# How densely the recurrence is issued beside attention and beside feed-forward

## The chip, the cores and the metric

The kernel runs on one core of a Trainium2 chip. The metric is the device time of one execution in microseconds (us); less is better. The core has five engines that work side by side, each through its own queue in order: TensorE (PE; its weight loads are listed as PEld), VectorE (DVE), ScalarE (ACT), GpSimd (POOL) and SyncE (SP), which here only issues transfers. They wait for one another by semaphores.

## The reference

Eight images of 384 channels and 32 x 32 pixels pass through two layers. Cut to what matters:

```python
# layer 0, for each batch, in both directions of the 1024 pixels
u, z   = split(rmsnorm(x) @ in_proj)
u      = silu(causal_conv4(u))
dt, Bm, Cm = split(u @ x_proj)
delta  = softplus(dt @ dt_proj + bias)
h      = exp(delta * A) * h + delta * u * Bm      # the recurrence, 16 states a channel
y      = (sum over states of h * Cm + u * D) * silu(z)
x      = x + res_scale * (scale_mod * (fwd + bwd) @ out_proj
                          + sigmoid(depthwise3x3(xn)) * xn)
# layer 1
t = t + attention(layernorm(t))                   # 6 heads, causal, 1024 tokens
t = t + feed_forward(layernorm(t))                # 384 -> 1536 -> 384, batches 0 to 4 only
```

The feed-forward scales its hidden values by the largest absolute value of the whole group (here one batch) before the GELU, and its output once more in the same way. So all hidden values of a batch must be there before the first GELU, and the GELUs before the second product.

## The kernel before

Everything is in float32, with channels on the 128 partitions (three blocks of 128) and the 1024 pixels or tokens along the free dimension, in two halves of 512. Four kinds of work are issued:

- **Preparation** of a batch (`before_scan`): norm, input projection (L342), the four-tap convolution, the 3 x 3 depthwise convolution on VectorE (`local`, L401), SiLU, the small projection (L489), and `delta` (L513 to L537), which ends with spilling delta and delta x u to DRAM. In `delta` the VectorE lines are L529 to L532.
- **The recurrence**, cut into 768 units, 96 a batch. A unit is one batch, one channel block, one direction and half, and two of the 16 states. `slot(k)` issues the stages of several units, each at its own lead: loads of rows (tile `bc`) and of `ud` and `dl`; `s_first` (GpSimd, L592) writes g = ud x B; `s_scan` has ScalarE make da = exp(delta x A) (L605), VectorE scan it (L610), and GpSimd multiply by C (L616); `s_sum` adds the states up in PSUM by eight transposes on TensorE (L624); `s_gate` finishes a block (L662 to L674). There are six g buffers; a unit's buffer comes free after its transposes. The GpSimd instructions are pinned to program order.
- **Attention** of a batch (`attention`): out-projection of the recurrence's result (L699), layernorm, projections (L729, L747), scores (L787), softmax, transposes (L863), weighted values (L877), projection (L937). It needs all 96 units of its batch.
- **Feed-forward** (`feed_forward`): layernorm, 24 half products of the first layer (`hp`, L995), `quant_scale` (L963 and around it), GELU and clamp (L1018, L1021), 6 half products of the second (`yp`, L1039), `quant_scale` again, the output.

The order of the batches is 0, 1, 2, 3, 5, 6, 4, 7; the first four and batch 4 have a feed-forward. The opening prepares the first four batches beside the first batch's units. Then comes the list `rest`: attention 0, feed-forward 0 joined with the preparation of batch 5, attention 1, feed-forward 1 joined with that of batch 6, and so on with 4 and 7; attention 5, attention 6, attention 4, and the feed-forward of 4 alone. The last attention runs by itself at the end.

Every step carries an assumed duration. `spread_over` merges two lists in proportion to these: each step stands at its middle, as a share of its list's total. The merged steps of a joint feed-forward are then multiplied by `JOINT`. The running sum of durations over `rest` is the planner's time. The units' slots are placed on it: `due` says by which planned time how many slots must be out, and from each point the planner takes the steepest line to any later due point and spaces the slots evenly along it. So a step that counts longer gets more slots beside it.

What is emitted in this order goes through a scheduler that may move instructions on each engine where data and buffers allow it, with a preference for the order of emission; a `high_priority` block goes ahead by the number it names, and pinned instructions keep their order among themselves. Which instruction stands where on an engine is settled before the run.

Of the kernel before, what the change touches and what calls it, by code (L numbers as in the profile page):

```python
# [38 lines left out]
BC0 = 32  # L39
DW = BC0 + 2 * NS  # L40
PARTS = ((0, 0), (0, 1), (1, 1), (1, 0))
JOINT = 0.6
SET = 8
HURRY = 400
AHEAD = 2
# [9 lines left out]
def kernel(  # L55
# [31 lines left out]
    def btile(name):  # L87
        return big.tile([P, NC, L], F32, name=name, tag="big")

    def mtile(name, n=L):  # L90
        return mid.tile([P, n], F32, name=name, tag="mid")
# [7 lines left out]
    def bank(name, tag=None):  # L99
        if tag is None:  # L100
            turn[0] += 1
            tag = ("s", "pt")[turn[0] % 2]
        return ps.tile([P, HB], F32, name=name, tag=tag, bufs=BANKS[tag])

    def half(h):
        return slice(h * HB, (h + 1) * HB)

    def chunk(c):
        return slice(c * P, (c + 1) * P)

    def load(dst, src):
        nc.sync.dma_start(out=dst, in_=src)
# [168 lines left out]
    def layernorm(src, name, emit):  # L281

        dst = src
        st = {}
        for h in range(NH):

            @emit.of(6.0)
            def _(h=h):
                mean = mean_of(lambda c: src()[:, c, half(h)], f"mean_{name}_{h}")
                for c in range(NC):  # L290
                    nc.vector.tensor_tensor(
                        dst()[:, c, half(h)], src()[:, c, half(h)], mean, ALU.subtract
                    )
                st[h] = squares(dst(), h, name)

        for h in range(NH):

            @emit.of(6.0)
            def _(h=h):
                var = mean_of(lambda c: st[h][c], f"var_{name}_{h}")  # L300
                rstd_of(var, 1)
                for c in range(NC):
                    nc.vector.tensor_tensor(  # L303
                        dst()[:, c, half(h)], dst()[:, c, half(h)], var, ALU.mult
                    )
# [652 lines left out]
    def quant_scale(mx, name):  # L958

        col = small.tile([P, 1], F32, name=f"col_{name}", tag="col")  # L960
        nc.vector.tensor_reduce(col, mx, AX.X, ALU.max)
        row = bank(f"row_{name}", "s")
        nc.tensor.transpose(row[:, :P], col.to_broadcast([P, P]), ident)  # L963
        s = small.tile([P, 1], F32, name=f"qs_{name}", tag="qs")
        nc.vector.tensor_reduce(s, row[:, :P], AX.X, ALU.max)
        nc.vector.tensor_scalar(s, s, QEPS, 1.0 / QMAX, ALU.add, ALU.mult)
        nc.vector.reciprocal(s, s)
        return s

    def feed_forward(b, t, emit):  # L970
        st = {}

        @emit
        def _():
            st["xn"] = t()
            st["mxh"] = small.tile([P, NF], F32, name=f"mxh_{b}", tag="mxh", bufs=1)
            st["mxy"] = small.tile([P, NC], F32, name=f"mxy_{b}", tag="mxy", bufs=1)

        layernorm(t, f"nf_{b}", emit)
        for m in range(NF):  # L980
            for h in range(NH):

                @emit.of(3.1)
                def _(m=m, h=h):
                    if m % NC == 0 and h == 0:
                        st["h", m // NC] = btile(f"h{m // NC}_{b}")
                    if m % 2 == 0 and h == 0:
                        st["w1"] = mtile(f"w1_{b}_{m}").rearrange("p (c e) -> p c e", c=4)
                        load(
                            st["w1"][:, :NC, :],  # L990
                            w1s[:, m * P : (m + 2) * P].rearrange("(c p) e -> p c e", p=P),
                        )
                    hp = bank(f"hp_{b}_{m}_{h}", "s")
                    for c in range(NC):
                        nc.tensor.matmul(  # L995
                            out=hp,
                            lhsT=st["w1"][:, c, chunk(m % 2)],
                            rhs=st["xn"][:, c, half(h)],
                            start=(c == 0),
                            stop=(c == NC - 1),  # L1000
                        )
                    hm = st["h", m // NC][:, m % NC, :]
                    nc.scalar.activation(hm[:, half(h)], hp, AF.Identity, bias=b1t[:, m : m + 1])
                    if h == NH - 1:
                        nc.vector.tensor_reduce(
                            st["mxh"][:, m : m + 1], hm, AX.X, ALU.max, apply_absolute_value=True
                        )

        @emit.of(3.0)
        def _():  # L1010
            st["s1"] = quant_scale(st["mxh"], f"h_{b}")


        @emit.of(3.0)
        def _():
            with tc.high_priority(offset=60):
                for q in range(NF // NC):
                    pin(nc.scalar.activation(st["h", q], st["h", q], AF.Gelu, scale=st["s1"]))  # L1018
                pin(nc.scalar.preload_act_table_set(LOG_EXP))
                for q in range(NF // NC):  # L1020
                    nc.vector.tensor_scalar(st["h", q], st["h", q], QCLIP, None, ALU.min)  # L1021

        for m in range(NC):
            for h in range(NH):

                @emit.of(10.7)
                def _(m=m, h=h):
                    if m == 0 and h == 0:
                        st["y"] = btile(f"yf_{b}")
                    if h == 0:  # L1030
                        for k in range(0, NF, 6):
                            w = mtile(f"w2_{b}_{m}_{k}", 6 * P).rearrange("p (k e) -> p k e", k=6)
                            load(
                                w, w2s[k * P : (k + 6) * P, chunk(m)].rearrange("(k p) e -> p k e", p=P)
                            )
                            st["w2", k // 6] = w
                    yp = bank(f"yp_{b}_{m}_{h}", "s")
                    for k in range(NF):
                        nc.tensor.matmul(  # L1039
                            out=yp,  # L1040
                            lhsT=st["w2", k // 6][:, k % 6, :],
                            rhs=st["h", k // NC][:, k % NC, half(h)],
                            start=(k == 0),
                            stop=(k == NF - 1),
                        )
                    ym = st["y"][:, m, :]
                    nc.scalar.activation(
                        ym[:, half(h)], yp, AF.Identity, bias=vec[:, m, V_B2 : V_B2 + 1]
                    )
                    if h == NH - 1:  # L1050
                        nc.vector.tensor_reduce(
                            st["mxy"][:, m : m + 1], ym, AX.X, ALU.max, apply_absolute_value=True
                        )

        @emit.of(3.0)
        def _():
            st["s2"] = quant_scale(st["mxy"], f"y_{b}")

        for m in range(NC):

            @emit
            def _(m=m):
                to = mtile(f"t3_{b}_{m}")
                load(to, spilled[b, "t2", m])
                for h in range(NH):
                    ym = bank(f"yq_{b}_{m}_{h}", "s")
                    nc.vector.tensor_scalar(
                        ym, st["y"][:, m, half(h)], st["s2"], QCLIP, ALU.mult, ALU.min
                    )
                    th = to[:, half(h)]  # L1070
                    nc.vector.scalar_tensor_tensor(th, ym, -QCLIP, th, ALU.max, ALU.add)
                nc.sync.dma_start(out=out[b, chunk(m), :], in_=to)


    class Steps(list):
# [4 lines left out]

        def of(self, us):
            return lambda f: self(f, us)

    def spread_over(*lists):

# [30 lines left out]
    def steps_of(stage, *args, **kwargs):  # L1116
        out = Steps()
        stage(*args, out, **kwargs)
        return out
# [30 lines left out]
    for i, b in enumerate(ORDER):  # L1150
        if i > 0:
            due.append((sum(us for _, us in rest), i * per))
        fed = Steps()
        rest += steps_of(attention, b, fed) if i < B - 1 else []
        if fed and later:
            fed = spread_over(fed, steps_of(before_scan, later.pop(0), ("pt", "pt", "av")))
            fed = [(f, JOINT * us) for f, us in fed]
        rest += fed

    timed, here = [], 0  # L1160
# [63 lines left out]
```

## Time and profile before

| what | us |
|---|---|
| median of 3 runs (lowest, highest) | 4947.52 (4943.62, 4969.08) |
| the profiled execution, its span | 4952.38, 4950.6 |
| PE, DVE, ACT, POOL busy in the span | 4007.3, 3659.0, 2669.5, 3696.7 |
| POOL L592 and L616, 768 each | 1843.2 and 1821.0 |
| DVE L610, 1536 scans | 907.5 + 953.7 |
| opening, up to the first L699 | 0 to 830 |
| first four periods, from one batch's L699 to the next batch's | 658, 675, 670, 682 |
| the last attention | from 4741 to the end |

The profile shows one execution. Busy time is the time in which an engine had an instruction at work; the rest is idle, and for each idle stretch the profile names the instruction or transfer whose end let the engine go on. Matmuls overlap each other on TensorE, so that its busy time is not its real load. "xN" counts instructions or, in a window, those at work in it; most TensorE products in float32 appear as two records each.

### The profile page before, as it was taken

How to read it: one execution, taken by the hardware profiler on the slowest of the kernel's cores; microseconds unless marked ns; L12 is line 12 of the kernel's file. 1: busy time of each engine (PE TensorE's matmuls, PEld its weight loads, DVE VectorE, ACT ScalarE, POOL GpSimd, SP SyncE). 2: the span in 40 equal slices, each digit the busy share in tenths (PEclk: the TensorE clock that was granted, in tenths of full speed). 3: DMA queues.
4: the chain of work that ended last, by engine and by line, in shares of the span. 5: the costliest groups of instructions: out<-in, count | busy, mean ns of one | idle time of the engine just before them, and what ended most of it. 6: DMA issues, size and time to landing. Idle time of an engine off the chain costs nothing. (4 is left out here: it accounts for less than half of the span.)

```text
span 4950.6 us, 50616 instructions
## 1 busy us (share of the span) xinstructions
PE 4007.3 (81%) x16362; PEld 2168.0 (44%) x16362; DVE 3659.0 (74%) x4818; ACT 2669.5 (54%) x4855; POOL 3696.7 (75%) x1944
## 2 busy tenths in 40 slices
PE   4677786988788788688887888887887988988889
PEld 1243343544444444344443444443454444444444
DVE  6887878677887778786778967687867677676623
ACT  4565655564654655545655446565456365464425
POOL 0487787996878986768876699867799888888800
PEclk7787796999989899888898998898899989989999
DMA  6554546333454334363343634334643334334210
GB/s 228 204 177 165 196 157 238 107 102 124 150 198 137 115 124 165 126 207 114 108 135 128 220 121 135 111 128 153 203 128 119 114 112 140 117 103 139 92 61 26
DMA packets 365009, 696.35 MB, mean 141 GB/s; under 512 B 30104, under 2 KB 88904, under 8 KB 364744
## 3 DMA queue, kind: packets, MB, share of 16 engines
q1 hardware_dynamic: 355232, 676.97, 41.4%
q10 hardware_dynamic: 9512, 16.15, 0.9%
q8 instruction: 129, 2.11, 0.2%
q14 instruction: 136, 1.11, 0.1%
HBM read 527.33 MB, written 165.68 MB: 140 GB/s over the span
## 5 line engine op out<-in xcount | busy, mean ns | idle before, releaser
L592 POOL TENSOR_TENSOR g<-ud,bc 128x1024 f32<-128x1024 f32 x768 | 1843.2, 2400 | 518.7 <-PE y L624 391.9
L616 POOL TENSOR_TENSOR g<-g,bc 128x1024 f32<-128x1024 f32 x768 | 1821.0, 2371 | 271.1 <-DVE g L610 196.1
L605 ACT ACTIVATE da<-dl,amat 128x512 f32<-128x512 f32 x1536 | 1056.9, 691 | 1457.7 <-DVE g L610 1436.7
L610 DVE TENSOR_TENSOR_SCAN g<-da,g 128x512 f32<-128x512 f32 x768 | 907.5, 1211 | 423.5 <-POOL g L592 411.8
L610 DVE TENSOR_TENSOR_SCAN g<-da,carry,g 128x512 f32<-128x512 f32 x768 | 953.7, 1272 | 348.4 <-POOL g L592 322.9
L624 PE MATMUL y<-ident,g 128*128 128x128 f32 x6144 | 938.7, 301 | 249.2 <-POOL g L616 122.2
L624 PEld LDWEIGHTS y<-ident,g 128*128 128x128 f32 x6144 | 782.0, 155 | 696.7 <-issue 379.8
L787 PE MATMUL s<-k,q 64*128 64x512 f32 (+3 forms) x1152 | 388.4, 600 | 121.6 <-DVE nm L801 103.5
L801 DVE CUSTOM_DVE_ANT_0 pr<-s,cmask 128x512 f32<-128x512 f32 (+3 forms) x576 | 300.3, 546 | 168.4 <-PE s L787 167.1
L811 ACT ACTIVATE pr<-pr,nm 128x512 f32<-128x512 f32 (+3 forms) x576 | 349.9, 609 | 123.6 <-DVE nm L801 121.9
L863 PE MATMUL pt<-ident,pr 128*128 128x128 f32 x1728 | 301.9, 307 | 98.1 <-ACT ptn L866 78.5
L995 PE MATMUL hp<-t,w 128*128 128x512 f32 x720 | 335.7, 611 | 38.7 <-DMA w<-w1s 30.8
L1039 PE MATMUL yp<-h,w 128*128 128x512 f32 x720 | 331.7, 619 | 19.2 <-DMA w<-w2s 15.1
L863 PEld LDWEIGHTS pt<-ident,pr 128*128 128x128 f32 x1728 | 216.2, 154 | 240.2 <-ACT ptn L866 134.5
L877 PE MATMUL av<-ptn,v 128*64 128x512 f32 (+3 forms) x1152 | 270.8, 551 | 49.7 <-ACT ptn L866 35.8
L342 PE MATMUL in<-xn,win 128*128 128x512 f32 x576 | 282.7, 637 | 26.8 <-DVE xc L464 8.2
L866 ACT COPY ptn<-pt 128x512 f32<-128x512 f32 (+3 forms) x576 | 255.6, 474 | 62.0 <-PE pt L863 60.0
L401 DVE SCALAR_TENSOR_TENSOR loc<-xn,vec,loc 128x496 f32<-128x496 f32 (+3 forms) x384 | 259.6, 722 | 20.1 <-ACT loc L390 18.8
L729 PE MATMUL qp<-t,wqk 128*128 128x512 f32 x576 | 263.3, 607 | 10.3 <-DVE t L303 6.5
L615 POOL COPY carry<-g 128x2 f32<-128x2 f32 x384 | 85.7, 223 | 214.8 <-DVE g L610 214.6
L787 PEld LDWEIGHTS s<-k,q 64*128 64x128 f32 x1152 | 132.2, 207 | 257.9 <-DVE nm L801 174.9
L1039 PEld LDWEIGHTS yp<-h,w 128*128 128x128 f32 x720 | 141.8, 201 | 194.0 <-issue 169.8
(151 smaller groups left out, 4714.2 us busy)
## 6 DMA issues: line engine op xcount, KB each, us to landing
bc<-rows SPq DMA_DIRECT2D x512, 512.0 KB, 4.2
dl<-sdl SPq DMA_DIRECT2D x160, 256.0 KB, 3.0
ud<-sud SPq DMA_DIRECT2D x160, 256.0 KB, 2.8
t<-st SPq DMA_DIRECT2D x63, 512.0 KB, 5.0
su<-u SPq DMA_DIRECT2D x48, 512.0 KB, 4.0
du<-su SPq DMA_DIRECT2D x96, 256.0 KB, 3.9
sdl<-du SPq DMA_DIRECT2D x96, 256.0 KB, 2.6
sud<-du SPq DMA_DIRECT2D x96, 256.0 KB, 2.2
```

The lines of the kernel that those rows point to most:

```text
L342: nc.tensor.matmul(out=mp, lhsT=st["win", c][:, k, i, :], rhs=st["xn"][:, k, half(h)], start=(k == 0), stop=(k == NC - 1),)
L592: pin(nc.gpsimd.tensor_tensor(g, ud, sst["bc", 0, u.b, u.part, u.n], ALU.mult))
L605: nc.scalar.activation(da, sst["dl", u.b, u.c, u.part], AF.Exp, scale=amat[:, u.c, n : n + 1])
L610: nc.vector.tensor_tensor_scan(gi[:, ::step], da[:, ::step], gi[:, ::step], first, ALU.mult, ALU.add)
L616: pin(nc.gpsimd.tensor_tensor(g, g, sst["bc", 1, u.b, u.part, u.n], ALU.mult))
L624: nc.tensor.matmul(out=y[:, j, :], lhsT=g[:, i, chunk(j)], rhs=ident, is_transpose=True, start=(u.opens and i == 0 and j == 0), stop=(u.cl ...
L787: mm = nc.tensor.matmul(out=ss[e][:, : k1 - k0], lhsT=st["q"][rows_of(e), c, chunk(qi)], rhs=st["k"][rows_of(e), c, k0:k1], start=True, st ...
L801: nc.vector.tensor_tensor_reduce(out=x, in0=ss[e][:, :w], in1=mask, scale=-1.0, scalar=-MASKED, op0=ALU.add, op1=ALU.min, accum_out=m,)
L811: nc.scalar.activation(x, x, AF.Exp, bias=m, scale=-1.0, accum_out=rs[:, i, e, kb : kb + 1])
L863: nc.tensor.transpose(pt[:, chunk(i)], pr[:, e, chunk(j % QT)], ident)
L995: nc.tensor.matmul(out=hp, lhsT=st["w1"][:, c, chunk(m % 2)], rhs=st["xn"][:, c, half(h)], start=(c == 0), stop=(c == NC - 1),)
L1039: nc.tensor.matmul(out=yp, lhsT=st["w2", k // 6][:, k % 6, :], rhs=st["h", k // NC][:, k % NC, half(h)], start=(k == 0), stop=(k == NF - 1),)
```

## The change

The factor on a joint feed-forward, `JOINT`, goes from 0.6 to 1.0. Three steps of the feed-forward, the two `quant_scale` calls and the GELU with its clamp, get the durations 9, 16 and 9 us in place of 3 each, and are marked as `Gap`. In `spread_over`, which merges the preparation of a later batch with the feed-forward, the longer durations count. After that merge a `Gap` step counts `SHORT` = 3.0 us for the slots. The last feed-forward, which has no preparation beside it, is not multiplied, and there the steps keep 9, 16 and 9 us. Nothing of what is computed changes.

```diff
-JOINT = 0.6
+JOINT = 1.0
+SHORT = 3.0
...
-        @emit.of(3.0)
+        @emit.of(Gap(9.0))
         def _():
             st["s1"] = quant_scale(st["mxh"], f"h_{b}")
...
-        @emit.of(3.0)
+        @emit.of(Gap(16.0))
         def _():
             with tc.high_priority(offset=60):
                 for q in range(NF // NC):
...
-        @emit.of(3.0)
+        @emit.of(Gap(9.0))
         def _():
             st["s2"] = quant_scale(st["mxy"], f"y_{b}")
...
+    class Gap(float):
+        pass
+
     def spread_over(*lists):
...
         if fed and later:
             fed = spread_over(fed, steps_of(before_scan, later.pop(0), ("pt", "pt", "av")))
-            fed = [(f, JOINT * us) for f, us in fed]
+            fed = [(f, JOINT * (SHORT if isinstance(us, Gap) else us)) for f, us in fed]
         rest += fed
```

## The prediction

> **What bounds the kernel now.** I read the page's slices first, then cut the span into stages, then asked each kind of stage who waits for whom. The slices, in fortieths of the span (124 us each):
>
> ```profile
> PE   4677786988788788688887888887887988988889
> DVE  6887878677887778786778967687867677676623
> POOL 0487787996878986768876699867799888888800
> ```
>
> No engine is full for long, and POOL (GpSimd) swings between 9 and 6 where DVE (VectorE) swings the other way. To see why, I cut where TensorE's timeline has the first out-projection matmul of a batch (L699) and its last attention-projection matmul (L937). From the first to the second I call an A stage (attention), from there to the next L699 an F stage (feed-forward, with a later batch's preparation beside it in the first four). The table by windows; its columns after the length are busy us of PE, PEld, DVE, ACT and POOL, then clock and DMA:
>
> ```profile
> 1488.00:1826.00 338.00, 279.92 (x1364) 159.55 (x1363) 247.97 (x362) 184.03 (x392) 297.21 (x154) 0.91 0.38 126
> 1826.00:2163.00 337.00, 266.17 (x889) 138.25 (x888) 271.50 (x299) 184.30 (x267) 230.74 (x119) 0.88 0.48 156
> 3857.00:4211.00 354.00, 296.45 (x1468) 171.64 (x1467) 250.92 (x366) 185.89 (x391) 319.21 (x167) 0.91 0.37 121
> 4211.00:4524.00 313.00, 267.65 (x1288) 150.86 (x1287) 213.82 (x326) 169.75 (x369) 268.73 (x147) 0.92 0.31 102
> 4524.00:4741.00 217.00, 183.44 (x659) 98.00 (x657) 131.83 (x128) 80.27 (x110) 151.36 (x70) 0.95 0.38 120
> 4741.00:4951.00 210.00, 199.70 (x864) 95.41 (x864) 66.12 (x201) 98.06 (x258) 0.00 (x0) 0.98 0.09 35
> ```
>
> These are A and F of batch 1, A of batches 6 and 4, F of batch 4, and the last batch's attention alone. In A, POOL is busy 297 of 338 us (88%) and DVE 73%. In F, POOL has 231 of 337 (68%) and DVE 81%. The waits of the first two windows say the same; first DVE's longest wait in A, then POOL's waits in F:
>
> ```profile
> DVE g L610 <- POOL g L592: 67.6, 44, 3.0
> ```
> ```profile
> POOL g L592 <- PE y L624: 40.1, 11, 7.1
> POOL carry L615 <- DVE g L610: 31.4, 4, 14.2
> POOL g L616 <- DVE g L610: 26.7, 3, 16.6
> ```
>
> In A the scans wait for POOL: POOL sets the pace. In F POOL waits: 40 us for transposes that free its g buffers, 58 us for scans that stand behind other DVE work, up to 16.6 us at once. So F has room on POOL, little on DVE, and that room is broken up by lumps of DVE work.
>
> The prices of a unit (two states of one channel block):
>
> ```profile
> L592 POOL TENSOR_TENSOR g<-ud,bc 128x1024 f32<-128x1024 f32 x768 | 1843.2, 2400 | 518.7 <-PE y L624 391.9
> L616 POOL TENSOR_TENSOR g<-g,bc 128x1024 f32<-128x1024 f32 x768 | 1821.0, 2371 | 271.1 <-DVE g L610 196.1
> ```
> ```profile
> 4664.52 23.44 PE yp L1039 x54
> 4700.44 1.75 PE y L624 x16
> ```
>
> POOL pays 2.40 + 2.37 us. DVE pays two scans, (907.5 + 953.7) / 768 = 2.42 us (the L610 groups of the page). TensorE's true price is in the chain of waits, where it runs without a pause: 1.75 / 16 = 0.109 us for a transpose, 0.87 us for the eight of a unit; 23.44 / 54 = 0.434 us for a 512-column record of the matmuls.
>
> **What the Trainium skill says.** "Perfetto Trace Analysis", Optimization Strategy: where the most contended engine changes between regimes, interleaving the regimes may help. The two windows above are such regimes. Identifying the Most-Contended Engine, same page: occupancy is a fair measure for the other engines, matmul busy time isn't for TensorE; hence my use of rates there. "SBUF — State Buffer", Who interferes with whom: a DVE operation with two SBUF inputs, or in a two-port mode, and a GpSimd operation that reads SBUF exclude each other; the later one waits for all of the earlier. The trace agrees: L530, with both inputs in SBUF, took
>
> ```profile
> L530 DVE SCALAR_TENSOR_TENSOR dp<-ew x96: 668/701/10682, 113.6 to 3518.9; 128x512 f32<-128x512 f32 x96
> ```
>
> that is 0.67 us at least and 10.7 at most, while L531, with one input in PSUM, never took over 0.69. "TensorE: Matmul & The Clock Gate", What's actually happening: the clock is throttled by default and activity releases it. The windows agree in direction: 0.98 in the last one, 0.88 to 0.91 where TensorE pauses. Denser work doesn't slow it.
>
> **The change, part by part.** It adds and removes no instruction of the computation; it moves units against the rest.
>
> Planner first. An attention counts 306.5 us, a feed-forward 181.6, a preparation 180.2. Before, a joint F counts 0.6 x 361.8 = 217.1. The steepest line to any due point then ends at the seventh batch: 576 / 2707.4 = 0.213 slots per planned us, 0.197 after it. Now a joint F counts 361.8 (the three gap steps 3 each), the steepest line is 672 / 3799.3 = 0.177, throughout. So an A gets 306.5 x 0.177 = 54 slots instead of 65, a joint F 64 instead of 46.
>
> A scheduler reorders afterwards, so I counted in the built order of TensorE, units between the same marks. A: 60, 60, 60, 62, 60, 70, 54 before and 50, 52, 52, 52, 52, 56, 52 after, 60 units fewer in all. F: 50, 52, 50, 52 before, 64, 68, 66, 66 after, 60 more, 15 a stage. The opening (102 units), the last F (36) and the last attention keep their counts. SP's loads of rows, ud and dl move with their units, about 15 more units' worth a joint F; DMA engines are busy 48% there, 38% in A, so I cost that at nothing; the cover goes if the w1 and w2 loads behind them come later than now (24 us of TensorE waits in F of batch 1).
>
> A stages: 7 of them, 2370 us in all (328, 338, 345, 350, 342, 354, 313). Their slope can be read off: 68 firsts on POOL (x of L592) gave 354 us, 57 gave 313, so 41 / 11 = 3.7 us a unit. 60 x 3.7 = 222 us. What is late next is TensorE: attention alone holds it 210 us, 53 units add 53 x 0.93 = 49 (0.87 and a share of the gate's transposes), 259 in stages that would last 307, 84% against 79% now. I take a tenth off: -200 us.
>
> Joint F stages: DVE has 271 us of work, 15 units add 36; POOL goes from 231 to 231 + 15 x 4.77 = 303. Exclusion takes more: L530 and L532 stand 24 times in a joint F, their means of 1.53 and 1.14 us are 0.65 us above the free 0.68; if the excess grows with POOL's share (68% to about 85%) plus clamps (L1021), some 10 us. DVE: 317 us. Its share is now 81%. I let it rise to 88%: in the new DVE order the stretches of over 6 us (by the durations of before) between two scans fall from 104 to 52, 98 to 55 and 104 to 63 us in F of batches 1 to 3 (batch 0 stays at 94), and these are the lumps POOL waits for. 317 / 0.88 = 360, +29 over the mean of 331: +116 us for four. Bounds: at 92%, which single 100 us slices reach, 345 (+14); at today's 82%, 387 (+56).
>
> The gap steps: 34 instead of 9 us of the feed-forward's inner length, so about 30 instead of 9 us of the preparation lie between quantization and GELU. TensorE is half idle there (14.1 of 30 us at 1993 to 2023), but POOL is already busy 27.2 of those 30: more in-projections fit, more units don't. It is part of the 88%. In the last F, without a preparation, the 25 planned us more only shift 36 units: nothing, bounded by -10 and +10.
>
> Sum: -200 + 116 = -84 on the profiled execution's 4952.4 us (span 4950.6): 4868. The median of the runs is 0.1% lower, so 4863; I say 4865.
>
> **Rivals.** *F absorbs nearly all.* For it: POOL idles 100 us in each joint F and the lumps halve. Against: DVE must reach 92%. -222 + 4 x 14 = -166: 4782.
> *A unit costs the same in both.* For it: the opening, also recurrence beside preparation, has POOL at 479 and DVE at 529 of the 630 us from 200 on, 76% and 84%. Against: its lumps are larger. F +52 each: -200 + 208 = +8: 4956.
> *Slower, by DVE's exclusion.* With POOL nearly without pauses, each of the 24 delta operations of a joint F ends behind a whole POOL operation (2.85 us, a length the L530 timeline shows again and again). 24 x (2.85 - 1.33) = 36 us instead of 10, and the scans queued behind them on the in-order DVE come later, and POOL for them: (271 + 36 + 36) / 0.88 = 390, +59 each: -200 + 236 = +36, 4983. It decides from +50 a joint F, that is some 29 us of added waiting. Against: in F of batches 1 and 2 over half of these operations were free.
>
> **How the numbers follow.** Forecast 0.42, own range 4820 to 4905. Absorbed 0.18, equal price 0.18, slower 0.22. The range of eight in ten, 4785 to 4978, takes in the ends 82% and 92% of DVE and leaves about 0.08 below and 0.12 above. A change under 0.5% (25 us) can't be told from none. Faster: 0.42 + 0.18 and a little of the equal price, 0.62; same 0.15; slower 0.23.
>
> **What would show it.** A stages near 310 us with POOL near 82%, and DVE's wait for L592 there well under 67 us; joint F stages near 360 with DVE at 88%, POOL near 84%; L530 mean under 2 us. It is wrong if A stages stay above 325 (then POOL wasn't their pace), or joint F stages pass 380 (then DVE had no room), by longer L530 and L532 or by waits on w1 and w2.

## The result, and the profile after

The changed kernel takes 4954.82 us (median of 8 runs, 4948.57 to 4962.85) against 4946.75 for the kernel before; the ratio is 1.0016, interval 0.9996 to 1.0037. No difference can be told. The profiled execution's span is 4950.7 us, to a tenth that of before. The forecast was 4865. Line numbers from here on are those of the kernel that is named; most of the changed kernel's are one higher than those of before (its L593 is L592 of before, its L617 is L616).

The slices of the page after, three engines:

```profile
PE   4687786988788888778888788887788898988889
DVE  6887878667877778886768786678867666676623
POOL 0487686887887888878878878787788788888700
```

POOL's swings are gone: mostly 7 and 8 where it had been 9 and 6. The work was spread as intended, and the time stayed. The table by windows, cut at the same marks (A and F of batch 1, A of batches 6 and 4, last F, last attention; columns as before):

```profile
1508.00:1832.00 324.00, 271.64 (x1317) 150.32 (x1318) 232.44 (x353) 176.00 (x382) 266.53 (x137) 0.93 0.37 123
1832.00:2189.00 357.00, 285.61 (x995) 154.75 (x993) 299.83 (x321) 208.27 (x302) 301.78 (x149) 0.88 0.50 163
3913.00:4226.00 313.00, 274.69 (x1344) 155.37 (x1343) 211.97 (x336) 170.04 (x367) 258.03 (x139) 0.94 0.38 124
4226.00:4526.00 300.00, 264.77 (x1296) 146.95 (x1295) 201.34 (x319) 165.48 (x367) 256.13 (x138) 0.95 0.30 99
4526.00:4741.00 215.00, 181.27 (x651) 99.06 (x648) 129.72 (x127) 80.78 (x111) 149.92 (x70) 0.92 0.37 119
4741.00:4951.00 210.00, 199.79 (x864) 95.47 (x864) 66.08 (x201) 98.06 (x258) 0.00 (x0) 0.98 0.09 35
```

All stages, from the first L699 start to the last L937 end for A, and from there to the next L699 for F:

| stages | before | after |
|---|---|---|
| A (7) | 331, 345, 354, 358, 342, 342, 320: 2392 | 314, 324, 338, 318, 331, 313, 300: 2238 |
| joint F (4) | 324, 328, 314, 328: 1294 | 363, 358, 370, 367: 1458 |
| last F | 211 | 215 |
| between batches 5, 6 and 4 | 12 | 2 |

A gave 154 us, the joint F stages took 164. In A of batch 1, the longest wait of DVE, then POOL's wait for the transposes that free its g buffers, before and after; last, POOL's waits in F of that batch:

```profile
DVE g L611 <- POOL g L593: 67.1, 41, 4.4
```
```profile
POOL g L592 <- PE y L624: 27.0, 14, 6.0
POOL g L593 <- PE y L625: 40.8, 22, 6.0
```
```profile
POOL carry L616 <- DVE g L611: 16.7, 5, 5.6
POOL g L593 <- PE y L625: 11.6, 6, 3.2
POOL g L617 <- DVE g L611: 11.0, 3, 4.6
```

In F POOL's three waits fell from 98 to 39 us. But POOL's work there rose by 75 (227 to 302 us, cut at the marks of the table), and this stage became 30 us longer. In A DVE waits for POOL as long as before, 67 us, though there are 8 units fewer, and POOL waits longer for TensorE. Over all seven A stages POOL's work fell by 286 us and its waits for the transposes rose from 212 to 340: nearly half of what the units left free came back as a wait for TensorE.

### The profile page after: what moved, and what is told of

It is laid out like the page before. It is cut to its first block, busy times and chain, and to the rows that moved or that the text cites. A ratio compares the mean times of both kernels' runs of the same rounds, so it can differ in the third digit from the quotient of the medians.

```text
span 4950.7 us, 50711 instructions
## 1 busy us (share of the span) xinstructions
PE 4013.9 (81%) x16362; PEld 2162.7 (44%) x16362; DVE 3618.6 (73%) x4808; ACT 2692.7 (54%) x4882; POOL 3696.0 (75%) x1944
## 4 chain that ended last, share of the span: by engine, by line
POOL 35%; PE 20%; DVE 20%; issue 16%; ACT 4%; DMA 4%; SPq 0%; ACTq 0%; POOLq 0%; DVEq 0%
POOL g L593 18%; POOL g L617 16%; DVE g L611 6%; PE qp L730 4%; PE y L625 3%; DVE loc L402 3%; PE yp L1040 2%; DVE dp L531 2%; PE s L788 2%; PE ap L938 2%; PE pt L864 1%; DVE u L371 1%; PE vp L748 1%; PE av L878 1%; DVE du L533 1%
## 5 line engine op out<-in xcount | busy, mean ns | idle before, releaser
L593 POOL TENSOR_TENSOR g<-ud,bc 128x1024 f32<-128x1024 f32 x768 | 1842.6, 2399 | 558.2 <-PE y L625 431.1
L617 POOL TENSOR_TENSOR g<-g,bc 128x1024 f32<-128x1024 f32 x768 | 1823.6, 2375 | 280.7 <-DVE g L611 165.5
L996 PE MATMUL hp<-t,w 128*128 128x512 f32 x720 | 350.1, 633 | 40.7 <-DMA w<-w1s 18.4
L996 PEld LDWEIGHTS hp<-t,w 128*128 128x128 f32 x720 | 137.9, 202 | 201.7 <-issue 146.9
```

The costliest lines, as they stand in the source:

```text
L593: pin(nc.gpsimd.tensor_tensor(g, ud, sst["bc", 0, u.b, u.part, u.n], ALU.mult))
L617: pin(nc.gpsimd.tensor_tensor(g, g, sst["bc", 1, u.b, u.part, u.n], ALU.mult))
L996: nc.tensor.matmul(out=hp, lhsT=st["w1"][:, c, chunk(m % 2)], rhs=st["xn"][:, c, half(h)], start=(c == 0), stop=(c == NC - 1),)
```

## Experiments

**The two parts of the change, and the split carried further.** `joint_only` has only the factor 1.0, `gap_only` only the gap steps; `joint_03` and `joint_16` are the kernel before and the changed one with another factor.

```diff
-JOINT = 0.6
+JOINT = 1.0   # joint_only: before; joint_03: 0.3
-JOINT = 1.0
+JOINT = 0.6   # gap_only: changed kernel; joint_16: 1.6
```

> The factor 1.0 without the longer gap steps: 367 units in A stages and 299 in F, as in the changed kernel (365 and 301). Equal price (a unit costs some 2.7 us in either stage, so moving it does nothing): 4945 to 4960. Parts that cancel (the move gains what the forecast says, the gap steps lose it again): 4860 to 4890.

> The longer gap steps with the factor left at 0.6: 426 and 240 units, as before (425 and 241). Equal price: 4930 to 4960, since only preparation moves into the gap. Parts that cancel: 5020 to 5050.

> The factor halved to 0.3: 494 and 173 units, 69 more in A. Equal price, throughout: 4950 within 25. Two limits with a flat middle (POOL in A, VectorE in F): A of 73 units needs 73 x 4.77 = 348 us of POOL, at the 89% of before 391 us, 47 more in six stages, F falls by some 24 in four: about 5130.

> The factor 1.6 with the gap steps: 299 and 367 units, 66 more in F than the changed kernel. Equal price, throughout: 4955 within 25. Two limits: F needs 300 + 18.5 x 2.42 = 345 us of VectorE, at its 83% 415 us, 52 more in four stages, and A stops falling at TensorE's 80%, (210 + 43 x 0.93) / 0.8 = 313, some 7 less in seven stages: about 5110.

| kernel | us | ratio to before, interval | mean units, A of batches 1 to 3 and joint F | mean A of batches 1 to 3 | mean joint F |
|---|---|---|---|---|---|
| joint_03 | 4992.0 | 1.0078 (1.0053 to 1.0104) | 72.8, 32.8 | 386 | 276 |
| before | 4950.0 | 1 | 61.9, 49.8 | 352 | 324 |
| gap_only | 4960.1 | 1.0019 (1.0009 to 1.003) | 62.6, 48.8 | 359 | 317 |
| joint_only | 4983.2 | 1.0061 (1.0044 to 1.0078) | 53.3, 66.0 | 327 | 373 |
| after | 4954.8 | 1.0016 (0.9996 to 1.0037) | 52.6, 65.5 | 327 | 364 |
| joint_16 | 5078.5 | 1.0251 (1.0218 to 1.0284) | 43.6, 83.8 | 310 | 430 |

(The ratio of the changed kernel is to the 4946.75 us of the kernel before as timed beside it.)

Read down, this is a price list. From row to row, a unit in A costs (386 - 352) / 10.8 = 3.1 us at the top, 26 / 9.3 = 2.7 between before and after, and (327 - 310) / 9.0 = 1.9 at the bottom. Over all seven A stages the factor alone took 58 units for 2392 - 2242 = 150 us, 2.6 each. In joint F stages it put in 65 units for 1493 - 1294 = 199 us, 3.1 each; from 33 to 50 units the price is 48 / 17 = 2.8, from 66 to 84 it is 65 / 18 = 3.6. The factor alone therefore loses, 33 us.

The gap steps give 1493 - 1458 = 35 us back in the joint F stages and cost 10 in the last F (205 to 215); they also shift units, 2 fewer in the joint F stages and 4 more in the last F. With the factor at 0.6 they also shorten the joint F stages (1294 to 1267), but A loses it (2392 to 2416, why is not shown), and the last F grows from 211 to 223. So "parts that cancel" was right with the signs turned, and the equal price is the sum of both parts.

The flat middle has limits on both sides, but the low one is soft: `joint_03` lost 42 us, more than the equal price allows (25) and far less than the two limits said (5130). `joint_16`, at 5078.5, came nearer to its limits (5110). The A and F of batch 2 of `joint_03`, and the same of `joint_16`:

```profile
2145.00:2530.00 385.00, 307.14 (x1497) 180.08 (x1498) 285.81 (x398) 200.15 (x415) 350.87 (x178) 0.88 0.39 129
2530.00:2809.00 279.00, 237.07 (x710) 116.25 (x708) 212.81 (x252) 156.46 (x226) 152.81 (x81) 0.91 0.44 150
```
```profile
2279.00:2592.00 313.00, 265.57 (x1271) 148.77 (x1271) 212.69 (x335) 170.65 (x373) 226.77 (x120) 0.92 0.36 118
2592.00:3019.00 427.00, 333.75 (x1155) 186.85 (x1153) 350.52 (x366) 231.91 (x333) 392.38 (x193) 0.81 0.47 157
```

POOL stands at 91% (351 of 385) in the A of the one and at 92% (392 of 427) in the F of the other: there it is at its fullest. VectorE's share of the joint F stages, by the same windows over all four, is 79% in `joint_03`, then 82% before, after and in `joint_16`: from 50 units on it doesn't rise with them. That looked like a bound at 82%, and was put to the test next.

**A unit's work taken away, engine by engine.** Each leaves a part of one engine's work of a unit out: a quarter of POOL's, half of VectorE's scans, or half of TensorE's transposes; the changed kernel first, then the kernel before. None of these computes the full result.

```diff
# pool_less, b_pool_less: C multiplies one of the two states
-        pin(nc.gpsimd.tensor_tensor(g, g, sst["bc", 1, u.b, u.part, u.n], ALU.mult))
+        bc1 = sst["bc", 1, u.b, u.part, u.n]
+        pin(nc.gpsimd.tensor_tensor(g[:, 0, :], g[:, 0, :], bc1[:, 0, :], ALU.mult))
# dve_less: s_scan's loop over two states; pe_less, b_pe_less: s_sum's
-        for i in range(2):
+        for i in range(1):
```

> The changed kernel, with L617 over one of a unit's two states only: 1.19 us less on POOL for every unit (C is not applied to the second state). VectorE paces F at 82% and TensorE A at 85%: F stays at 355 to 365, A at 310 to 320, in all 4900 to 4955. POOL's pace in both: F falls from 364 by 66 x 1.19 to 286, A from 320 by 52 x 1.19 to 258, in all about 4300.

> The changed kernel, with one of a unit's two scans and one of its two exponentials left out (the second state stays unscanned): 1.21 us less on VectorE, 0.69 less on ScalarE for every unit. VectorE paces F: its work falls from 300 to 220, the next limit is POOL, 303 / 0.91 = 333 us, 31 less in each joint F; A stays within 8 of 320; in all, with some 60 less in the opening, about 4770. POOL's pace in both: F and A within 8 of 364 and 320, in all 4920 to 4960.

> The changed kernel, with the transposes of one of a unit's two states left out (the second state is not summed): 0.44 us less on TensorE for every unit. TensorE paces A at 85%: A falls by 52 x 0.44 / 0.85 = 27 to 293, F stays at 360 to 365, in all about 4770. POOL's or VectorE's pace in A: within 8 of 320, in all 4930 to 4960.

> The kernel before, with L616 over one of a unit's two states only, 1.19 us less on POOL for every unit. POOL alone sets the pace of A before (the prediction's step): A of 62 units falls until TensorE stops it, (210 + 62 x 0.93) / 0.85 = 315, that is by 30 or more in each. POOL and TensorE share it, as in the changed kernel, where 62 us less on POOL gave 21: 62 x 1.19 x 0.33 = 24 each. F of 50 units falls by 0.38 x 60 = 23.

> The kernel before, with the transposes of one of a unit's two states left out, 0.44 us less on TensorE for every unit. POOL alone sets the pace of A before: A within 5 of 344, in all 4930 to 4955. TensorE holds A as it does in the changed kernel (1.06 us for each us taken): A falls by 62 x 0.44 x 1.06 = 29 in each, in all about 4750. F unchanged in both.

| kernel | us | A: taken from a stage, stage shorter by | joint F: taken, shorter by |
|---|---|---|---|
| pool_less | 4617.8 | 62, 21 | 78, 30 |
| b_pool_less | 4558.9 | 72, 31 | 60, 26 |
| pe_less | 4779.8 | 23, 24 | 29, 1 |
| b_pe_less | 4830.2 | 27, 20 | 22, longer by 2 |
| dve_less | 4909.3 | 63, 2 | 80, 5 |

(Taken: mean units by 1.19, 0.44 or 1.21 us. `dve_less` also takes 0.69 us a unit from ScalarE.) `pe_less` came in where TensorE paces A, and `dve_less` just below the range in which POOL paces both; `pool_less` and `b_pe_less` fell between their two expectations. The F of batch 1 of `dve_less`:

```profile
1793.00:2156.00 363.00, 284.14 (x1007) 154.63 (x1005) 236.63 (x262) 168.98 (x238) 309.79 (x151) 0.87 0.50 163
```

VectorE fell from 84% to 65% and the stage didn't get shorter. So the scans don't pace F, and "VectorE at its cap" falls. (In `dve_less` the built order put 6 units more into the joint F stages; corrected for them the scans give about 0.12 us of F for each us taken instead of 0.06.) POOL does in part: 0.38 to 0.43 us of F for each us taken, and neither the scans nor the transposes make up the rest. In A TensorE matters as much: 1.06 us for each us of transposes in the changed kernel and 0.75 already in the kernel before, beside 0.33 and 0.43 for POOL.

`b_pool_less` alone would speak for POOL as the pace of A: its A stages fell by 31 us, as the first expectation said (30 or more), and end with TensorE busy 88%. `b_pe_less` decides: with POOL's work untouched A fell by 20, where POOL alone allowed 5. The traces show the way. POOL's waits for the transposes in A fell from 212 to 31 us in all, while the A stages became 139 shorter; in `pe_less` they fell from 340 to 136, and A by 169. So POOL had not set A's pace alone: it stood waiting for TensorE to free its buffers. Whether TensorE's whole load or the time of the transposes alone makes it wait, these runs don't separate.

These prices have limits. The cut on POOL is a large one, and in `pool_less` another engine is near its end, TensorE with 89% in A and VectorE with 89% in F; the first us taken from POOL may be worth more than the mean. The granted clock moved with the cuts, from 0.886 in the changed kernel to 0.913 in `pool_less` and 0.858 in `pe_less`; its part in the prices is not separated. And they don't explain all: a unit's 4.77 us on POOL, 0.88 on TensorE and 2.42 on VectorE at these prices make about 2.6 us in A, as measured, but only 2.0 to 2.2 in F, where the factor alone cost 3.1. The rest of a unit's price in F is open; transfers, and ScalarE alone, were not varied.

**The other work of F.** `loc_less` leaves out the four corner taps of the 3 x 3 filter, `yp_less` every other hidden block of the second product.

```diff
-                if k == 4:
+                if k in (0, 2, 4, 6, 8):      # loc_less, in local
-                    for k in range(NF):
+                    for k in range(0, NF, 2): # yp_less
```

> The changed kernel, with the four corner taps of the 3 x 3 filter left out: 24 operations of 0.68 us less on VectorE in each preparation, all of them in the lumps in which no scan can run. The lumps hold F, though the scans don't: F falls by 16 in each, and the opening by up to 50, in all about 4850. VectorE doesn't hold F in any way: F within 5 of 364, in all 4940 to 4960.

> The changed kernel, with the second feed-forward product over every other hidden block (half of the sum is left out): 36 x 2 records of 0.434 us less, 31 us of TensorE, in every feed-forward; the planner's order puts 63 instead of 66 units in F. TensorE's own long products hold F, though the transposes don't: F falls by 31 and 8 for the three units, to 325. They don't: F at 355 to 364, only the last F falls, by up to 31.

`loc_less`: 4900.1 us. The joint F stages are 1433 instead of 1458, 6 each for 16 taken, 0.39 of it; the opening is 33 shorter. This lies between the two expectations, and is the same share as POOL's. `yp_less`: 4906.1 us. Joint F 1406, 13 each, of which the three units fewer account for about 9; so 31 us of TensorE's long products bring some 4, nearer to the second expectation. The last F fell by 26. POOL's time and VectorE's lumps, then, each hold F for a part, TensorE hardly, the scans hardly. One reading is a chain through queues that each run in order; the runs don't show it apart from others.

**VectorE's exclusion by POOL.** `excl` keeps w and the difference of delta in PSUM, so that no operation of `delta` has two SBUF inputs.

```diff
+            w = bank_of(f"wp{d}_{b}_{c}_{h}")
-            nc.vector.tensor_tensor(dl, dl, dp, ALU.subtract)
-            nc.vector.tensor_tensor(u, u, dl, ALU.mult)
+            nc.vector.tensor_tensor(w, dl, dp, ALU.subtract)
+            nc.vector.tensor_tensor(u, u, w, ALU.mult)
+            nc.scalar.copy(dl, w)
```

> The changed kernel, with w and the difference that L532 forms kept in PSUM, so that neither L531 nor L533 has two SBUF inputs, and a copy of 0.58 us on ScalarE for each delta. VectorE paces F and its exclusion by POOL is part of that: L531 and L533 fall from 1.43 and 1.10 us to 0.7, 24 operations in a joint F give 24 x 0.57 / 0.82 = 17 us, 67 in all, some 40 more in the opening: about 4850. The exclusion costs nothing, since the waits only move: 4940 to 4970.

It took 5016.8 us, ratio 1.0136 (1.0103 to 1.0169), longer than either expectation. The operations did fall, from 1.43 and 1.10 to 0.68 and 0.67 us, yet VectorE now waits 45.8 us for ScalarE before the first operation of `delta` (18.9 in the changed kernel), the opening took 27 us more, and the built order put 71 units instead of 66 in the joint F stages. A gain that these hide can't be excluded; that the exclusion is what holds F is not supported.

**Work moved off POOL, and the split in the middle.** `mid8` has the factor 0.8, and spares the last F the longer steps. `carry_dve` and `carry_act` take the small copy of the carry (L616) from POOL to VectorE or ScalarE, `mul4` moves every fourth unit's multiplication by C to VectorE; `mul4cm` is `mid8`, `carry_dve` and `mul4` together, `carry_act8` is `mid8` and `carry_act`.

```diff
-JOINT = 1.0
+JOINT = 0.8                                                  # mid8
-        rest += fed
+        rest += [(f, SHORT if isinstance(us, Gap) else us) for f, us in fed]
-            pin(nc.gpsimd.tensor_copy(carry[:, u.n : u.n + 2], g[:, :, end]))
+            nc.vector.tensor_copy(carry[:, u.n : u.n + 2], g[:, :, end])  # carry_dve
+            nc.scalar.copy(carry[:, u.n : u.n + 2], g[:, :, end])         # carry_act
+        if units.index(u) % 4 == 3:                          # mul4
+            nc.vector.tensor_tensor(g, g, bc1, ALU.mult)
```

> The changed kernel with the factor 0.8, and the gap steps counting 3 for the slots in the last feed-forward too: 397 units in A and 269 in joint F stages and the last F, between the two kernels. The split doesn't matter in the middle and the gap steps gain some 30 us in the joint F stages and lose 10 in the last F, both as the runs before showed: 4925 to 4945. The two kernels already stand at the bottom whatever the gap steps do: 4945 to 4960.

> The changed kernel with L616's copy of the carry on VectorE instead of POOL: 85.7 us less on POOL, some 25 more on VectorE. Both stages pay for POOL's time (0.33 to 0.43 us for each us) and hardly for the scans' time on VectorE (0.06): 85.7 x 0.38 = 33 less, 4915 to 4930. VectorE paces F (the prediction's sum): 4950 to 4975.

> The changed kernel with every fourth unit's multiplication by C (L617) on VectorE: 192 x 2.37 = 455 us less on POOL, 192 x 1.22 = 234 more on VectorE (1.22 as L440 takes for the same size when POOL leaves it alone). Paid for at the prices that the runs showed (0.38 and 0.06): 455 x 0.38 - 234 x 0.06 = 159 less, about 4795. VectorE paces F, and its exclusion by POOL lengthens the moved operations: 16 x 1.22 / 0.82 = 24 more in each joint F, A some 10 less in each: 4980 or more.

> The three edits of mid8, carry_dve and mul4 together. If POOL's time is what a unit costs and the gains add: 4955 - 20 - 33 - 159 = about 4745. If VectorE takes over as the bound once it has this work: above 4850.

> The changed kernel with the copy of the carry (L616) on ScalarE: 81.5 us less on POOL, some 384 x 0.2 = 77 us more on ScalarE. POOL's time is paid for, and carry_dve lost only because VectorE's small copy waited for POOL (0.95 us instead of 0.12): 81.5 x 0.38 = 31 less, 4915 to 4930. Work moved off POOL gains nothing wherever it goes, since the hand-over between engines costs as much: 4945 or more.

> mid8 with the copy of the carry on ScalarE. The gains add: 4931 - 31 = 4900. As above otherwise: 4925 or more.

| kernel | us | ratio to before, interval |
|---|---|---|
| mid8 | 4931.1 | 0.9964 (0.9953 to 0.9975) |
| carry_dve | 5020.8 | 1.0146 (1.0123 to 1.0169) |
| mul4 | 4994.0 | 1.0095 (1.0077 to 1.0114) |
| mul4cm | 5028.3 | 1.0170 (1.0150 to 1.0191) |
| carry_act | 4919.2 | 0.9936 (0.9912 to 0.9961) |
| carry_act8 | 4911.8 | 0.9921 (0.9890 to 0.9953) |

`mid8` came in as its first expectation said: A 2321, joint F 1365, last F 209. The two moves to VectorE failed: `mul4` by its second expectation, `carry_dve` slower than both of its own. The groups of the copy in `carry_dve` and in `carry_act`, and the tile's line for the moved multiplication in `mul4`:

```profile
L616 DVE COPY carry<-g 128x2 f32<-128x2 f32 x384 | 363.7, 947 | 5.9
```
```profile
L616 ACT COPY carry<-g 128x2 f32<-128x2 f32 x384 | 73.6, 192 | 195.0 <-DVE g L611 190.2 <-DVE rs L832 1.9 <-DVE col_h L962 1.6
```
```profile
L619 DVE TENSOR_TENSOR g<-g,bc x192: 1191/2176/3442, 206.3 to 4748.8; 128x1024 f32<-128x1024 f32 x192
```

A copy of two columns, 0.117 us at best, took VectorE 0.947 us in the mean; the multiplication took 2.2 us instead of 1.19. "SBUF — State Buffer" of the Trainium skill, Who interferes with whom, names copies in a two-port mode and operations with two SBUF inputs among those that can contend with POOL; the runs agree. In the trace of `carry_dve` the 139 copies beside which POOL was idle took at most 0.172 us, and all 230 that took over 0.2 us ended 0.02 to 0.03 us after the end of a POOL instruction. On ScalarE the same copy took 0.175 to 0.212 us, always, and the 36 us gained (4954.8 to 4919.2) are near the 31 expected. So POOL's price, 0.38, held in this one move to an engine that doesn't contend; with `mid8` the gains add in part, 4912 for 4900. Of the versions that compute the full result `carry_act8` has the lowest median and beats the kernel before by 0.8%; its lead over `carry_act` is within the spread of the runs. `mul4cm` went past the 4850 that was to show VectorE as the bound: against `mid8`, its A stages took 2392 us instead of 2321, its joint F stages 1379 instead of 1365.

## Why the prediction was wrong

- **Planner and counts: right.** 60 units moved, 15 to each joint F, as counted; POOL at 82% in A (266.5 of 324) and 85% in F of batch 1.
- **A stages, -200: measured -154.** The failed term is the slope, "41 / 11 = 3.7 us a unit", taken at nine tenths: "what is late next is TensorE", and its part was put at that one tenth. The slope was read off two stages of one trace that differ in more than units: A of batch 4 went from 320 to 300 us with about 2 units fewer. Measured, a unit moved out of A is worth 154 / 60 = 2.6, and 3.1 even where POOL is fullest (`joint_03`). Behind it stands the step "POOL sets the pace": in the kernel before, 72 us less of POOL gave 31 and 27 us less of TensorE gave 20. The sign in the profile was that POOL had 12% of idle time in A of batch 1, 41 us, and 27.0 of it was waiting for transposes. The prediction read this wait in F and not in A. Of its signs, POOL near 82% came; DVE's wait for POOL well under 67 us did not, nor A near 310 (320 in the mean).
- **Joint F, +116: measured +164.** The stages became 364 us, near the 360 forecast, but the base was 324, not 331: the windows of the prediction ended A with the start of the last projection's group and F a few us late. That is 7 of the 12 us a stage. The rest is "I let it rise to 88%": VectorE's share stayed at 80 to 85%, and `dve_less` shows that the scans' work was not the measure. That 364 lies so near 360 is luck: 317 us of VectorE's work at 88% were forecast, 300 at 82% measured. That the lumps shrink was right (the stretches of over 6 us between two scans fell from 480 to 309 us in the four stages), and POOL's waits fell by 59 us in F of batch 1; what came in their place is TensorE waiting for POOL at the transposes (5.0 us before, 41.7 after).
- **Gap steps, "part of the 88%": undersized.** They give 35 us in the joint F stages, some 6 of it by 2 units fewer, and without them the change loses. Their cost in the last F, 10 us by `joint_only`, lay at the edge of the bound.
- **The rivals.** The equal price (4956) came true as a sum, with both of its terms too large: -200 and +208 were set against -154 and +164, about 2.6 us a unit in either stage once the gap steps are counted in. The slower case by exclusion is not what the trace shows: the mean of L530 (L531 after) fell from 1.53 to 1.43 us although POOL was denser in F.
- **Costed at nothing, and rightly:** the w1 and w2 loads. TensorE's waits for them fell from 24 to 5 us in F of batch 1.

## What to carry to other kernels

The stages here had several engines at 70 to 90% and no single bound, and an engine's share of busy time didn't say what a unit of work costs there. Making POOL even over the two kinds of stages brought nothing by itself. Take a part of the work away on one engine at a time and see how much of it the stage gives back; or compare the same stage at two amounts of work, never two unlike stages of one trace. Moving work between two stages gains only the difference of these prices, here 2.6 against 3.1 us, and near equal prices the split hardly matters. Where an engine that seems to set the pace still idles a tenth of the time, look at what it waits for: in A it was TensorE, and it set the pace with POOL.

## What the runs showed of the hardware

How much POOL holds up small operations on VectorE wasn't expected: the copy of 128 x 2 values took from 0.117 to 2.377 us there, 0.599 in the median, and 0.193 in the median on ScalarE. Moving 82 us of copies off POOL to VectorE cost 66 us of run time; moving them to ScalarE gained 36. An input in PSUM ended it here: the operation of L531 took 0.666 to 10.691 us in the changed kernel and, with one of its inputs moved to PSUM, 0.667 to 0.700 us in `excl`.

The prediction said that the later of the two waits for all of the earlier, and that the 10.7 us of L530 agree. But 10.7 us is more than one such wait, for the longest POOL instruction took 3.9 us. In the kernel before, this operation stood through four more POOL instructions that began after it:

```profile
2768.90 10.68 DVE L530 SCALAR_TENSOR_TENSOR dp<-ew 128x512 f32<-128x512 f32 x1
2769.76 2.37 POOL L616 TENSOR_TENSOR g<-g,bc 128x1024 f32<-128x1024 f32 x1
2772.07 2.36 POOL L592 TENSOR_TENSOR g<-ud,bc 128x1024 f32<-128x1024 f32 x1
2774.37 2.36 POOL L616 TENSOR_TENSOR g<-g,bc 128x1024 f32<-128x1024 f32 x1
2776.66 2.36 POOL L592 TENSOR_TENSOR g<-ud,bc 128x1024 f32<-128x1024 f32 x1
```

It was rare: 2 of the 192 executions of L530 and L532 took over 2.9 us.
